# A written slot order for TensorE, VectorE and ScalarE in the message stage of a graph network kernel

## The chip, the core and the metric

The kernel runs on one core of a Trainium2 chip. The metric is the device time of one execution in microseconds (us). The kernel before takes 4433.76 us, the median of three timed runs that lie between 4427.78 and 4445.74 us. The profile is one more execution, taken by the hardware profiler; its span is 3774.9 us.

A core has five engines[...]: TensorE (PE in the profile: matrix products and transposes, results into PSUM), VectorE (DVE), ScalarE (ACT), GpSimd (POOL, which here issues the gathers by index) and SyncE (SP, which here issues the plain DMA transfers). [...]

## The reference

The input is a graph of 6250 nodes with 64 features and 206250 edges, sorted by destination. Four layers follow, each with a residual: x becomes x + layer(relu(layernorm(x))). The first, second and fourth multiply by the normalised adjacency matrix, with weights in the first, and three times in the fourth. The third layer is the one this study is about. Cut to what matters:

```python
Vp = leaky_relu(h @ pAw + pAb) @ pBw + pBb            # per node
x  = relu(relu(E @ w1 + b1) @ w2 + b2)                # per edge, E is 206250 x 64
msg = sigmoid(x @ Bw + Bb) * Vp[src] + (x @ Cw + Cb)  # per edge
M = clip(msg, 1e-5) ** 2
mean = segment_sum(M, dst) / max(count, 1)
out = sqrt(mean)                                      # per node
```

## The kernel before

The kernel first builds the 6272 x 6272 matrix of edge counts as bf16 tiles in device memory (`A`, 14 strips), multiplying by it as it goes, then makes two further products with it (to 1125 us in the profile), then does the third layer (**the message stage**), then the rest of the fourth layer's three products. A float32 operand of such a product is split into three bf16 terms (`split`), so that bf16 products sum to it.

**The message stage** is the loop at L1192. It goes over G = 202 groups of 1024 edges, that is J = 8 edges on each of 128 partitions. For one group:

- `v`: eight gathers by index on GpSimd (L1195), each fetching 128 rows of `Vp_dram`; four buffers.
- `e`: the edge features, one DMA on SyncE (L1199).
- `p_e`: four transposes on TensorE (L1203), copied out by ScalarE to `eT` (L1205).
- `p_1`, `h1`, `p_2`, `h2`: two products with block-diagonal weights (L1207, L1211), each taken out of PSUM by ScalarE with a relu (L1209, L1213).
- `p_bc`: gates and shifts, a product with the biases and one with the weights (L1216, L1220), over two PSUM banks.
- `gate`: a sigmoid on ScalarE (L1223).
- `m`: on VectorE the product with `v`, the shift and the clip (L1225 to L1227).
- `m3`: the square split into three bf16 terms, by ScalarE (L1229, L1230, L1232) and VectorE (L1231, L1233) in turn.
- `to`: VectorE's comparison of node numbers with the edges' destinations (L1238), a one-hot matrix over one or two blocks of 128 nodes.
- `p_s`: TensorE sums the messages into their nodes with it (L1246); a block that is complete is taken out to `H` (L1250). After each seventh block, `finished` does the square root, the residual and the layer norm of a chunk of 896 nodes.

**The matrix work beside it.** A list `todo` holds work on the adjacency matrix that does not depend on the group: `piece` loads a tile of `A`; `crossed` transposes a part of it on TensorE into the PSUM bank `p_sum` (L1136) and has VectorE compare it with the opposite tile (L1139), which is the check that the matrix is symmetric; `partial` multiplies a tile with a chunk that is complete (L732, called from L1144) and has VectorE add the result to `Y` (L1150, L1152), which is part of the fourth layer's first product. `p_sum` is one bank, so each of these must be read before the next begins. There are 196 `crossed`, 84 `partial` and 92 `piece` entries. `some_of` does a share per group, so that the list is empty when the next chunk is complete. The chunks' last groups are 29, 58, 87, 116, 145, 174 and 201.

**What sets the order.** The program names for each instruction its engine and its operands. A scheduler of the framework then fixes, at compile time, the order in each engine's queue from the dependencies and its own priorities, and adds the semaphores. PSUM has eight banks, and the stage uses all: `p_e`, `p_1`, `p_2`, `p_sum` one each, `p_bc` two, `p_s` two. SBUF tiles have three buffers each, `v` four. A tile can be written again when its last reader is done.

Of the kernel before, what the change touches and what calls it, by code (L numbers as in the profile page):

```python
# [8 lines left out]
F32 = mybir.dt.float32  # L9
BF16 = mybir.dt.bfloat16  # L10
FP16 = mybir.dt.float16
I32 = mybir.dt.int32
AF = mybir.ActivationFunctionType
OP = mybir.AluOpType
AX = mybir.AxisListType

P = 128
# [562 lines left out]

K1 = EP // P
LOOK = 101
NS = K1 // LOOK * P
# [11 lines left out]
def window(g):  # L597

    per = N / E
    lo = max(int(g * P * J * per) - DRIFT, 0) // P  # L600
    hi = min(int((g + 1) * P * J * per) + DRIFT, NP - 1) // P
    return lo, hi - lo + 1
# [3 lines left out]
def fast(ctx, tc, bad, x, src, dst, edge_attr, W3, b3, W4, b4, w1, b1, w2, b2, Bw, Bb, Cw, Cb,  # L606
# [432 lines left out]
    with ExitStack() as ph:  # L1039
# [83 lines left out]
        def crossed(n, i, k, b):  # L1123
            if b % ROWS == 0:
                held["there"] = mpool.tile([P, ROWS, 2, CW], BF16, name="there", bufs=2)
                m = min(ROWS, CB - b)
                for h in range(2):
                    nc.sync.dma_start(held["there"][:, :m, h, :],
                                      A[2 * i + h][:, k * CB + b:k * CB + b + m, :])

            p = ps_a.tile([P, 512], F32, name="p_sum").bitcast(BF16).rearrange(
                "p (a q) -> p a q", q=P)[:, :CB, :]
            for q in (slice(0, P),) if b != CB // 2 else (slice(0, D), slice(D, P)):
                half, lo = divmod(b * P + q.start, CW)
                for a in range(CB):
                    nc.tensor.transpose(p[q, a, :], held[half][:, a, lo:lo + q.stop - q.start],  # L1136
                                        ident_b)
            junk = mpool.tile([P, CB * P], BF16, name="junk", bufs=1)
            nc.vector.scalar_tensor_tensor(  # L1139
                junk, p.rearrange("p a q -> p (a q)"), 0.0,  # L1140
                held["there"][:, b % ROWS].rearrange("p h w -> p (h w)"), op0=OP.add,
                op1=OP.not_equal, accum_out=unlike[:, n:n + 1])

        def partial(i, s):  # L1144

            p = ps_a.tile([P, 512], F32, name="p_sum")
            for b in range(CB):
                spread(p, U3, i * CB + b, held[s % 2][:, b, :], CW, i * CB, CB)
            if i == 0:
                nc.vector.tensor_copy(Y[:, s, :], p[:, :CW])  # L1150
            else:
                nc.vector.tensor_add(Y[:, s, :], Y[:, s, :], p[:, :CW])  # L1152

        todo, crossings = [], []

        def plan(pairs, sums):
            order = [k for i, k in pairs] + [k for k in range(NC) if (pairs[-1][0], k) not in pairs]
            for at, (i, k) in enumerate(pairs if not sums else [(pairs[0][0], k) for k in order]):
                for half in range(2):
                    todo.append((piece, i, 2 * k + half))  # L1160
                    if sums:
                        todo.append((partial, i, 2 * k + half))
                    if at < len(pairs):
                        for b in range(3 + half) if not half else range(3, CB):
                            todo.append((crossed, len(crossings), i, k, b))
                            crossings.append((i, k, b))

        def some_of(left):

            n = -(-len(todo) // max(left, 1))  # L1170
            for _ in range(n):
                f, *args = todo.pop(0)
                f(*args)

        def finished(c):

# [12 lines left out]
        last = {b: g for g in range(G) for b in range(window(g)[0], sum(window(g)))}  # L1189
        ends = [last[c * CB + CB - 1] for c in range(NC)]  # L1190
        acc = {}
        for g in range(G):  # L1192
            v = mpool.tile([P, J, D], F32, name="v", bufs=4)
            for j in range(J):
                nc.gpsimd.indirect_dma_start(  # L1195
                    out=v[:, j, :], out_offset=None, in_=Vp_dram[:, :],
                    in_offset=bass.IndirectOffsetOnAxis(ap=src_g[:, g, j:j + 1], axis=0))
            e = mpool.tile([P, J * D], F32, name="e")
            nc.sync.dma_start(  # L1199
                e, edge_attr[g * P * J:(g + 1) * P * J, :].rearrange("(p j) f -> p (j f)", j=J))  # L1200
            p_e = ps_a.tile([P, 512], F32, name="p_e")
            for k in range(J // 2):
                nc.tensor.transpose(p_e[:, k * P:(k + 1) * P], e[:, k * P:(k + 1) * P], ident)  # L1203
            eT = mpool.tile([P, 512], F32, name="eT")
            nc.scalar.activation(eT, p_e, AF.Copy)  # L1205
            p_1 = ps_a.tile([P, 512], F32, name="p_1")
            nc.tensor.matmul(p_1, w1_d, eT, start=True, stop=True)  # L1207
            h1 = mpool.tile([P, 512], F32, name="h1")
            nc.scalar.activation(h1, p_1, AF.Relu, bias=b1_c)  # L1209
            p_2 = ps_a.tile([P, 512], F32, name="p_2")  # L1210
            nc.tensor.matmul(p_2, w2_d, h1, start=True, stop=True)  # L1211
            h2 = mpool.tile([P, 512], F32, name="h2")
            nc.scalar.activation(h2, p_2, AF.Relu, bias=b2_c)  # L1213
            p_bc = ps_a.tile([P, J, 2, D], F32, name="p_bc")
            for b in range(2):
                nc.tensor.matmul(p_bc[:, 4 * b:4 * b + 4].rearrange("p j o f -> p (j o f)"), ones,  # L1216
                                 BC_b, start=True, stop=False)
                for k in range(2):
                    q = 2 * b + k
                    nc.tensor.matmul(p_bc[:, 2 * q:2 * q + 2].rearrange("p j o f -> p (j o f)"),  # L1220
                                     h2[:, q * P:(q + 1) * P], BC, start=False, stop=(k == 1))
            gate = mpool.tile([P, J, D], F32, name="gate")
            nc.scalar.activation(gate, p_bc[:, :, 0, :], AF.Sigmoid)  # L1223
            m = mpool.tile([P, J, D], F32, name="m")
            nc.vector.tensor_mul(m, gate, v)  # L1225
            nc.vector.tensor_add(m, m, p_bc[:, :, 1, :])  # L1226
            nc.vector.tensor_scalar_max(m, m, EPS)  # L1227
            m3 = mpool.tile([P, J, 3, D], BF16, name="m3")
            nc.scalar.activation(m3[:, :, 0, :], m, AF.Square)  # L1229
            nc.scalar.activation(m, m, AF.Square)  # L1230
            nc.vector.tensor_sub(m, m, m3[:, :, 0, :])  # L1231
            nc.scalar.activation(m3[:, :, 1, :], m, AF.Copy)  # L1232
            nc.vector.tensor_sub(m3[:, :, 2, :], m, m3[:, :, 1, :])  # L1233

            some_of(min(k for k in ends if k >= g) + 1 - g)
            b0, nb = window(g)
            to = mpool.tile([P, 2 * P, J], BF16, name="to")
            nc.vector.tensor_tensor(  # L1238
                to[:, :nb * P, :], count[:, :nb * P, :],
                rel_b[:, g, :].unsqueeze(1).to_broadcast([P, nb * P, J]), op=OP.is_equal)  # L1240
            for b in range(b0, b0 + nb):
                begins = b not in acc
                if begins:
# [5 lines left out]
                if last[b] == g:  # L1249
                    nc.vector.tensor_reduce(  # L1250
                        H[:, b, :], acc[b][:, :3 * D].rearrange("p (t f) -> p f t", f=D),
                        axis=AX.X, op=OP.add)
                    if b % CB == CB - 1:
                        finished(b // CB)

        assert not todo and len(crossings) == 28 * CB

# [99 lines left out]
```

## Time and profile before

| stretch of the profile, us | what runs | length, us |
|---|---|---|
| 0 to 615 | building the matrix, first product | 615 |
| 615 to 1125 | two products with the matrix | 510 |
| 1125 to 3279 | message stage | 2154 |
| 3279 to 3775 | rest of the fourth layer | 496 |

| engine | busy in the whole span, us | share |
|---|---|---|
| TensorE | 3173.7 | 84% |
| VectorE | 1845.4 | 49% |
| ScalarE | 1329.9 | 35% |
| GpSimd | 1723.4 | 46% |

How to read what follows: a row of the costliest groups names the line, engine and operation, the tiles written and read, the count, the busy time and mean nanoseconds of one, and the idle time just before with what ended it. "issue" is idle time for which the profile shows no wait. A row of the timeline has the start, the duration, the engine and the operation, and in brackets the idle time before it and what ended that. A row of waits reads "who <- for whom", with the total, the number of times and the longest. [...]

### The profile page before, as it was taken

How to read it: one execution, taken by the hardware profiler on the slowest of the kernel's cores; microseconds unless marked ns; L12 is line 12 of the kernel's file. 1: busy time of each engine (PE TensorE's matmuls, PEld its weight loads, DVE VectorE, ACT ScalarE, POOL GpSimd, SP SyncE). 2: the span in 40 equal slices, each digit the busy share in tenths (PEclk: the TensorE clock that was granted, in tenths of full speed). 3: DMA queues.
4: the chain of work that ended last, by engine and by line, in shares of the span. 5: the costliest groups of instructions: out<-in, count | busy, mean ns of one | idle time of the engine just before them, and what ended most of it. 6: DMA issues, size and time to landing. Idle time of an engine off the chain costs nothing.

```text
span 3774.9 us, 59396 instructions
## 1 busy us (share of the span) xinstructions
PE 3173.7 (84%) x24499; PEld 1907.5 (51%) x24499; DVE 1845.4 (49%) x3013; ACT 1329.9 (35%) x2120; POOL 1723.4 (46%) x1822
## 2 busy tenths in 40 slices
PE   0499998999967777888878888888888888799999
PEld 0366665555534444444544444454444454466665
DVE  5999992221124445555555554555555455430000
ACT  0477771100104434334434434443443434310000
POOL 4100000000017777777777777777777777500000
PEclk9999998999978889889989889889899999899999
DMA  3244446968894333343434334333233333499987
GB/s 108 80 181 180 180 180 276 421 276 347 315 168 128 85 81 104 82 129 90 119 100 120 101 99 127 93 114 112 81 112 116 104 113 93 142 338 376 371 352 298
DMA packets 278031, 650.47 MB, mean 172 GB/s; under 512 B 106505, under 2 KB 158787, under 8 KB 275699
## 3 DMA queue, kind: packets, MB, share of 16 engines
q1 hardware_dynamic: 220036, 584.91, 42.9%
q0 software_dynamic: 54112, 58.92, 7.3%
q8 instruction: 194, 3.18, 0.3%
q10 hardware_dynamic: 3600, 2.73, 0.3%
q14 instruction: 89, 0.73, 0.1%
HBM read 562.82 MB, written 83.58 MB: 171 GB/s over the span
## 4 chain that ended last, share of the span: by engine, by line
POOL 32%; PE 15%; issue 12%; DMA 8%; DVE 2%; ACT 1%; POOLq 0%; DVEq 0%
POOL v L1195 32%; PE p_sum L732 11%; DMA v<-Vp_dram,src_g 7%; PE p_node L723 1%; PE p_bc L1220 1%; DMA piece<-A 1%; PE p L1207 1%; PE p L1211 0%; PE p_s L1246 0%; DVE m L1225 0%; PE p_sum L1136 0%; DVE junk L1139 0%; PE p_bc L1216 0%; DVE m L1226 0%; DVE m L1231 0%
## 5 line engine op out<-in xcount | busy, mean ns | idle before, releaser
L1195 POOL DMA_INDIRECT v<-Vp_dram,src_g x1616 | 1662.5, 1029 | 528.3 <-issue 455.2
L732 PE MATMUL p_sum<-piece,U 128*64 128x448 bf16 x10290 | 1083.7, 359 | 46.3 <-DVE junk L1139 22.9
L732 PEld LDWEIGHTS <-U 128*64 128x64 bf16 x12348 | 688.1, 111 | 610.8 <-issue 172.2
L1220 PE MATMUL p_bc<-BC,h 128*128 128x256 f32 x1616 | 507.5, 437 | 19.1 <-ACT h L1213 18.8
L1082 POOL MEMSET origin<- 128x4 f32 (+3 forms) x49 | 1.7, 100 | 968.3 <-PE p_sum L732 968.3
L1225 DVE TENSOR_TENSOR m<-gate,v 128x512 f32<-128x512 f32 x202 | 139.6, 691 | 510.9 <-DMA v<-Vp_dram,src_g 424.5
L1220 PEld LDWEIGHTS p_bc<-BC,h 128*128 128x128 f32 x1616 | 300.3, 207 | 173.7 <-issue 84.8
L1246 PE MATMUL p_s<-m,to 128*128 128x192 bf16 x2816 | 293.0, 259 | 73.8 <-DVE m L1233 73.7
L1246 PEld LDWEIGHTS <-to 128*128 128x128 bf16 x2816 | 270.6, 147 | 130.8 <-issue 124.3
L938 ACT ACTIVATE strip<-p_a 128x784 bf16<-128x784 f32 x392 | 301.6, 820 | 90.9 <-PE p_a L934 89.5
L1216 PE MATMUL p_bc<-BC_b,ones 3*128 3x512 bf16 x404 | 168.7, 418 | 190.0 <-DVE m L1226 188.4
L1229 ACT ACTIVATE m<-m 128x512 bf16<-128x512 f32 x202 | 126.9, 628 | 444.2 <-DVE m L1227 443.6
L1238 DVE TENSOR_TENSOR to<-count,rel_b 128x2048 bf16<-128x2048 bf16 (+1 forms) x202 | 218.8, 1084 | 101.8 <-PE p_s L1246 100.7
L973 ACT ACTIVATE y<-p_sum 128x448 f32<-128x448 f32 x56 | 30.5, 544 | 674.8 <-PE p_sum L732 674.8
L1207 PE MATMUL p<-eT,w_d 128*128 128x512 f32 x404 | 246.8, 696 | 25.3 <-ACT eT L1205 24.9
L1139 DVE SCALAR_TENSOR_TENSOR junk<-p_sum,there 128x896 bf16<-128x896 bf16 x196 | 213.1, 1087 | 78.6 <-PE p_sum L1136 69.9
L1211 PE MATMUL p<-h,w_d 128*128 128x512 f32 x404 | 240.7, 680 | 8.3 <-ACT h L1209 7.3
L1223 ACT ACTIVATE gate<-p_bc 128x512 f32<-128x512 f32 x202 | 120.6, 597 | 351.3 <-PE p_bc L1220 351.1
L925 DVE TENSOR_TENSOR lo<-count,key 128x2048 bf16<-128x2048 bf16 x196 | 238.2, 1215 | 0.0
L732 PE MATMUL p_sum<-strip,U 128*64 128x448 bf16 x2058 | 236.6, 358 | 0.4 <-ACT strip L938 0.4
L1231 DVE TENSOR_TENSOR m<-m,m 128x512 f32<-128x512 f32 x202 | 139.7, 691 | 168.8 <-ACT m L1230 168.8
L934 PE MATMUL p_a<-hd,lo 128*128 128x98 bf16 x3136 | 190.2, 214 | 33.1 <-DVE lo L925 31.8
(173 smaller groups left out, 3012.8 us busy)
## 6 DMA issues: line engine op xcount, KB each, us to landing
piece<-A SPq DMA_DIRECT2D x498, 784.0 KB
A<-strip SPq DMA_DIRECT2D x14, 5488.0 KB
e<-in_edge_attr SPq DMA_DIRECT2D x202, 256.0 KB
v<-Vp_dram,src_g POOLq DMA_INDIRECT x1616
there<-A SPq DMA_DIRECT2D x56, 448.0 KB
there<-A SPq DMA_DIRECT2D x56, 336.0 KB
pairs<-pair SPq DMA_DIRECT2D x1, 1616.0 KB
Vp_dram<-v SPq DMA_DIRECT2D x7, 224.0 KB
```

The costliest lines, as they stand in the source:

```text
L732: nc.tensor.matmul(p[half * D:(half + 1) * D, :w], U3[:, b, k, :], at_block, start=(i < 2), stop=(i >= 3 * n - 2))
L925: nc.vector.tensor_tensor(t, of.unsqueeze(1).to_broadcast(t.shape), key[:, k, at:at + GB].rearrange("p (h j) -> p h j", j=GQ) .unsqueeze(2 ...
L934: nc.tensor.matmul(p[:, j, :2 * NB], lo[:, g // GQ, :, g % GQ], hd[:, g // GQ, :, g % GQ], start=True, stop=True)
L938: nc.scalar.activation(strip[:, :, col:col + 2 * SG].rearrange("p b (j l) -> p b j l", l=2), p[:, :, :2 * NB].rearrange("p j (b l) -> p b ...
L1139: nc.vector.scalar_tensor_tensor(junk, p.rearrange("p a q -> p (a q)"), 0.0, held["there"][:, b % ROWS].rearrange("p h w -> p (h w)"), op0 ...
L1195: nc.gpsimd.indirect_dma_start(out=v[:, j, :], out_offset=None, in_=Vp_dram[:, :], in_offset=bass.IndirectOffsetOnAxis(ap=src_g[:, g, j:j ...
L1207: nc.tensor.matmul(p_1, w1_d, eT, start=True, stop=True)
L1211: nc.tensor.matmul(p_2, w2_d, h1, start=True, stop=True)
L1216: nc.tensor.matmul(p_bc[:, 4 * b:4 * b + 4].rearrange("p j o f -> p (j o f)"), ones, BC_b, start=True, stop=False)
L1220: nc.tensor.matmul(p_bc[:, 2 * q:2 * q + 2].rearrange("p j o f -> p (j o f)"), h2[:, q * P:(q + 1) * P], BC, start=False, stop=(k == 1))
L1238: nc.vector.tensor_tensor(to[:, :nb * P, :], count[:, :nb * P, :], rel_b[:, g, :].unsqueeze(1).to_broadcast([P, nb * P, J]), op=OP.is_equal)
L1246: nc.tensor.matmul(acc[b][:, :3 * D], to[:, (b - b0) * P:(b - b0 + 1) * P, j], m3[:, j].rearrange("p t f -> p (t f)"), start=(begins and j ...
```

## The change

The loop over groups becomes functions, one for each step, and a loop over slots calls them. In slot i each step works on another group: the transposes on group i, the first layer on i - 1, the second on i - 2, the gates on i - 3, sigmoid, clip and squares on i - 4 (`M_AT`), the sums into nodes on i - 5 (`SUM_AT`). So what a step needs from another engine was made in the slot before, with a few exceptions inside the slot. There are G + 5 slots. The whole loop stands in a region in which TensorE, ScalarE and VectorE issue in exactly the order in which the program names their instructions; GpSimd and SyncE are still the scheduler's. The matrix work is done in two shares a slot, and its reading by VectorE is put off to named places (`read_them`). The list's due times (`ends`) move by five slots, and a tile's `crossed` entries now come ahead of its `partial`. The edge features are loaded two slots ahead. Its aim is that no engine waits at the head of its queue for something that another has only just been given to do.

```diff
+ET = mybir.EngineType
...
+            def compared():
+                junk = mpool.tile([P, CB * P], BF16, name="junk", bufs=1)
+                nc.vector.scalar_tensor_tensor(...)
+            return compared
...
-        def some_of(left):
-            n = -(-len(todo) // max(left, 1))
-            for _ in range(n):
+        def some_of(n):
+            for _ in range(min(n, len(todo))):
                 f, *args = todo.pop(0)
-                f(*args)
+                if f is not piece:
+                    read_them()
+                then = f(*args)
+                if then:
+                    read.append(then)
...
+        BC_AT, M_AT, SUM_AT = 3, 4, 5
+        ends = [e + SUM_AT for e in ends]
...
-            nc.vector.tensor_sub(m, m, m3[:, :, 0, :])
-            nc.scalar.activation(m3[:, :, 1, :], m, AF.Copy)
-            nc.vector.tensor_sub(m3[:, :, 2, :], m, m3[:, :, 1, :])
-            some_of(min(k for k in ends if k >= g) + 1 - g)
...
+        def slot(i):
+            def at(later):
+                return 0 <= i - later < G
+            if i + 2 < G:
+                loaded(i + 2)
+            if at(3):
+                evicted(i - 3, "p_2", "h2", func=AF.Relu, bias=b2_c)
+            if at(M_AT):
+                gated(i - M_AT)
+                clipped(i - M_AT)
+            if at(0):
+                fetched(i)
+                turned_edges(i)
+            read_them()
+            if at(1):
+                layer(i - 1, w1_d, "eT", "p_1")
+            if at(M_AT):
+                squared(i - M_AT)
+            n = -(-len(todo) // max(min(k for k in ends if k >= i) + 1 - i, 1))
+            some_of(n - n // 2)
+            if at(M_AT):
+                compared_nodes(i - M_AT)
+                m, m3 = of[i - M_AT].pop("m"), of[i - M_AT]["m3"]
+                nc.vector.tensor_sub(m, m, m3[:, :, 0, :])
+                nc.scalar.activation(m3[:, :, 1, :], m, AF.Copy)
+            if at(2):
+                layer(i - 2, w2_d, "h1", "p_2")
+            if at(BC_AT):
+                gates_and_shifts(i - BC_AT)
+            if at(0):
+                evicted(i, "p_e", "eT", func=AF.Copy)
+            if at(1):
+                evicted(i - 1, "p_1", "h1", func=AF.Relu, bias=b1_c)
+            if at(M_AT):
+                nc.vector.tensor_sub(m3[:, :, 2, :], m, m3[:, :, 1, :])
+            read_them()
+            some_of(n // 2)
+            if at(SUM_AT):
+                summed(i - SUM_AT)
+
+        loaded(0)
+        loaded(1)
+        with tc.manual_schedule(engines={ET.PE, ET.Activation, ET.DVE}):
+            for i in range(G + SUM_AT):
+                slot(i)
+            read_them()
```

## The prediction

> **What bounds the kernel now.** I read the busy table by stage first, because the page's shares mix stages with different limits. Columns: stretch and length, busy time of TensorE, its weight loads, VectorE, ScalarE and GpSimd (each with a count), granted TensorE clock, DMA share, GB/s.
>
> ```profile
> 1125.00:3279.00 2154.00, 1775.79 (x9770) 1037.36 (x9771) 1130.31 (x1814) 895.28 (x1459) 1661.59 (x1616) 0.90 0.37 106
> 3279.00:3775.00 496.00, 469.89 (x4721) 287.87 (x4719) 75.80 (x131) 37.20 (x65) 0.83 (x1) 0.98 0.89 342
> ```
>
> The first row is the message stage, the only one the diff touches: 2154 of 3775 us. No engine looks full there: TensorE 82%, GpSimd 77%. Next the costliest group on GpSimd, on the page and then by itself (shortest, median, longest ns; first and last start):
>
> ```profile
> L1195 POOL DMA_INDIRECT v<-Vp_dram,src_g x1616 | 1662.5, 1029 | 528.3 <-issue 455.2
> L1195 POOL DMA_INDIRECT v<-Vp_dram,src_g x1616: 941/947/2005, 1124.9 to 3278.9; - x180
> ```
>
> The 1616 row gathers run from the first to the last microsecond of the stage, and their idle time is nearly all "issue", a wait for nothing. The GpSimd timeline shows what that is:
>
> ```profile
> 2212.14 0.95 POOL L1195 DMA_INDIRECT v<-Vp_dram,src_g  x1 [0.30 <-issue]
> 2213.39 1.50 POOL L1195 DMA_INDIRECT v<-Vp_dram,src_g  x1 [0.31 <-issue]
> 2215.20 0.95 POOL L1195 DMA_INDIRECT v<-Vp_dram,src_g  x1 [0.30 <-issue]
> ```
>
> Each gather is 0.95 us, with 0.30 us to the next, always. So GpSimd takes one every 1.25 us with no pause: 1616 x 1.25 = 2020 us, plus the lengthened ones (mean 1029 against median 947 ns, x 1616 = 133 us), gives 2153 of the 2154 us. GpSimd sets the stage, at 2154/202 = 10.66 us a group. The waits of the stage say the same from the other side (total, times, longest, us):
>
> ```profile
> DVE m L1225 <- DMA v<-Vp_dram,src_g: 423.1, 119, 8.1
> ACT m L1229 <- DVE m L1227: 439.7, 150, 7.9
> PE p_bc L1216 <- DVE m L1226: 188.4, 82, 7.0
> PE p_s L1246 <- DVE m L1233: 66.5, 32, 5.1
> ```
>
> VectorE waits for gathered rows, ScalarE for VectorE, TensorE for VectorE: one wait passed on. Last, how the stage ends:
>
> ```profile
> 3282.06 0.69 DVE L1225 TENSOR_TENSOR m<-gate,v 128x512 f32<-128x512 f32 x1 [1.42 <-DMA v<-Vp_dram,src_g]
> ...
> 3287.43 1.44 PE L1246 MATMUL p_s<-m,to 128*128 128x192 bf16 x8 [7.14 <-DVE m L1233]
> ```
>
> The last gather issues at 3278.9, its product starts 3.2 us later, the last sum 5.4 us after that.
>
> One thing the page does not explain: the timed runs take 4433.76 us against a profiled span of 3774.9, a factor of 1.17. [...] No run here shows the clock of the timed runs; I assume all engines slowed together, GpSimd still sets the stage, and a microsecond of the profile is worth 1.17 in the timed run.
>
> [...] 431 gathers with no VectorE operation beside them average 0.946 us; 71 with only the node comparison (L1238) beside them average 1.26. [...] the chain shows 2.4 us from issue to data again and again.
>
> **The change, part by part.**
>
> *GpSimd and DMA work.* The same 1616 gathers into the same four `v` buffers; the same loads. 0 us off the 2020 us floor.
>
> *The order on three engines.* No arithmetic is added or removed; per group TensorE does 1775.79/202 = 8.79 us, VectorE 1130.31/202 = 5.60, ScalarE 895.28/202 = 4.43, all under 10.66. What must be asked is whether the fixed order holds an engine longer than 10.66 us a slot. TensorE: from the first share of matrix work in a slot (it needs its `p_sum` bank read) round to the same place in the next lies one group's work, 8.79 us; it then waits about 1.9 us for VectorE to clip and read. VectorE: clip 0.69 + 0.68 + 0.46, a read of `p_sum` 1.17 (or 0.61), comparison 1.09, subtraction 0.69, ScalarE's copy 0.63 and about 0.15 of hand-over, subtraction 0.69: 6.3 us. ScalarE does nothing in a slot that it must wait for longer than that. Queued behind VectorE's wait for `v` are the `p_sum` reads, hence TensorE's matrix work, hence the gates: all delayed, none for longer than the gathers take. Cost in steady state 0; GpSimd's gathers hide it.
>
> *The distance of four slots to the product.* `fetched(i)` needs the buffer whose reader is `clipped(i-4)`. Three further buffers are 3 x 10.66 = 32 us of gathers; the product starts 2.4 us after its data's issue. About 29 us of slack. At the start, four buffers are free for 43 us from 1124.9, and slots 0 to 3 have at most 4 x 8.79 = 35 us of TensorE work. Cost 0, with 8 us to spare.
>
> *The ends of the seven chunks.* `finished` runs from L1250 to the last split in 10.6 us (3288.90 to 3299.52), and the written order puts the next slot's clip behind it. Within 29 us of slack, regained at 1.9 us a slot: 0. If none were hidden: 6 x 10.6 = 64 us.
>
> *The tail.* The last sum moves into slot 206, behind two more shares of the matrix work (a partial sum is some 2 us, a transposed comparison 0.7 us plus 1.17 of reading): 2 to 6 us, take 4; x 1.17 = 5.
>
> [...] Of the 133 us of lengthening the comparison makes most. It stays one per group, but its place after `v` arrives becomes nearly fixed, so its phase against the gathers is no longer spread. In the trace it lengthens gathers by some 0.1 us where it starts in the first 0.3 us of a gather's period and by 0.7 to 0.9 near its end; the slot's three possible places (0, 0.61 or 1.17 us of reading before it) fall in different phases. I take no change; ends -50 and +50 us.
>
> Sum: 4433.8 + 5 = 4438 us.
>
> **Rivals.** (1) [...] The same floor, and 2/5 of the 133 us go: 53 x 1.17 = 62, so 4376 us. For: the fixed place. Against: three phases average out. (2) *TensorE paces the timed runs.* If the factor 1.17 lies in TensorE's clock alone, 8.79 us a group becomes over 10.66 and its order counts. Its waits on ScalarE and VectorE outside the `p_bc` one sum to 184 us (66.5 on L1246, 25 on L1207, 26 on L1220 and L1211, 67 on `p_sum`); half of them x 1.17 = 108, so 4330 us. For: the granted clock of 0.90 here. Against: 0.96 to 0.99 in the other stretches, so the clock would have to fall everywhere. (3) *The written order costs.* Chunk ends unhidden and tail, (64 + 5) x 1.17 = 81: 4515 us. For: VectorE and ScalarE can no longer slip the next group's work between `finished`'s steps. Against: the 29 us of slack.
>
> **How the numbers follow.** Forecast 0.45, rival 1 0.17, rival 2 0.17, rival 3 0.21. Within 0.5% (22 us) lies most of the forecast's case: 0.42, with 0.02 to the faster side and 0.01 to the slower, so faster 0.36, slower 0.22. The range runs from 4320, which takes in rival 1 and half of rival 2, to 4515, which takes in half of rival 3; 0.08 + 0.10 are left out.
>
> **What would show it.** Right: 1616 gathers still 1.25 us apart with idle "issue" only, first to last start 2154 us apart within 25, the last sum 8 to 12 us after the last product starts. Rival 1: mean gather near 1.00 us. Rival 3: GpSimd waiting for VectorE (L1225) at chunk ends. Wrong altogether: a timed gain with a profiled gather stretch unchanged, which would mean that the timed runs are paced by something other than in the profile.

## The result, and the profile after

The changed kernel takes **4268.65 us** (median of four runs, 4252.64 to 4271.52) against 4439.75 us of the kernel before in the same series: ratio 0.9591, 95% interval 0.9523 to 0.9659. It is 171 us faster.

In some series of runs the kernel before takes about 3780 us and in others 4350 to 4450 us, all runs of a series alike, so kernels are compared only within a series. I call these the 3780 and the 4430 (or upper) level: the profile of before (3774.9 us) is of the first, and its timed runs, the timed runs of the changed kernel and the profile of after are of the second.

The busy table by stage of the changed kernel, with the columns of the prediction's first fence:

```profile
0.00:615.00 615.00, 460.03 (x5522) 300.99 (x5522) 518.11 (x865) 350.23 (x505) 51.98 (x59) 0.95 0.37 149
615.00:1125.00 510.00, 468.36 (x4482) 279.77 (x4483) 113.90 (x199) 47.18 (x91) 8.71 (x147) 0.95 0.87 316
1125.00:3770.00 2645.00, 1911.13 (x9735) 1117.82 (x9734) 1165.96 (x1821) 871.60 (x1448) 1632.38 (x1616) 0.80 0.32 86
3770.00:4267.00 497.00, 475.12 (x4762) 290.00 (x4762) 76.46 (x131) 36.59 (x64) 0.00 (x0) 0.98 0.89 343
```

Three stages last what they lasted before (615, 510 and 497 us). All of the excess over 3775 us lies in the message stage, 2645 us, and there VectorE, ScalarE and GpSimd have nearly the busy times of the profile of before (within 3.2%). What differs is idle time and the granted TensorE clock, 0.80 against 0.90. So the factor of 1.17 is not a slower clock of every engine.

The gathers, from the page's costliest groups and by themselves (shortest, median, longest ns, first and last start):

```profile
L1226 POOL DMA_INDIRECT v<-Vp_dram,src_g x1616 | 1632.4, 1010 | 1019.9 <-DVE m L1261 510.6
L1226 POOL DMA_INDIRECT v<-Vp_dram,src_g x1616: 939/945/1959, 1132.5 to 3748.0; - x180
```

A gather still takes 0.945 us, but GpSimd now waits 510.6 us for VectorE's product to free a `v` buffer, which it never did in the profile of before. TensorE's part of the timeline (PE its products and transposes, PEld its weight loads) shows another engine that is slow:

```profile
2297.33 0.14 PEld L1286 LDWEIGHTS <-to 128*128 128x128 bf16 x1 [1.97 <-issue]
2298.04 0.32 PE L1286 MATMUL p_s<-m,to 128*128 128x192 bf16 x1 [1.78 <-issue]
2298.77 0.15 PEld L1286 LDWEIGHTS <-to 128*128 128x128 bf16 x1 [1.29 <-issue]
2299.46 0.32 PE L1286 MATMUL p_s<-m,to 128*128 128x192 bf16 x1 [1.10 <-issue]
2300.16 0.18 PEld L1234 LDWEIGHTS p_e<-ident,e 128*128 128x128 f32 x1 [1.24 <-issue]
2300.86 0.37 PE L1234 MATMUL p_e<-ident,e 128*128 128x128 f32 x1 [1.08 <-issue]
```

One instruction starts every 0.70 us, whichever it is, and none waits for another engine ("issue"). In the stage TensorE has 546 idle times of over 0.15 us that no wait explains, 419 us in all; after 404 of them the instruction starts about 0.7 or 1.4 us after the one before. The profile of before, at the 3780 level, has two such idle times in the stage, of 5.9 and 0.4 us, both in its first 2.2 us.

### The profile page after: what moved, and what is told of

The parts are those of the page before. It is cut to its first block, busy times and chain, and to the rows that moved or that the text cites. A ratio compares the mean times of both kernels' runs of the same rounds, so it can differ in the third digit from the quotient of the medians.

```text
span 4266.6 us, 59486 instructions
## 1 busy us (share of the span) xinstructions
PE 3314.6 (78%) x24499; PEld 1988.6 (47%) x24499; DVE 1874.4 (44%) x3013; ACT 1305.6 (31%) x2108; POOL 1693.1 (40%) x1822
## 4 chain that ended last, share of the span: by engine, by line
PE 56%; DVE 13%; issue 13%; another core or an unknown queue 8%; ACT 4%; DMA 3%; POOL 2%; DVEq 0%; ACTq 0%; SPq 0%; POOLq 0%
PE p_sum L733 28%; PE p_bc L1252 7%; PE p L1238 6%; PE p_s L1286 5%; PE p_a L935 3%; PE p_bc L1248 2%; DVE junk L1143 2%; DVE m L1261 2%; PE p_node L724 2%; PE p_e L1234 2%; DVE m L1262 2%; PE p_sum L1137 1%; POOL v L1226 1%; ACT h L1242 1%
## 5 line engine op out<-in xcount | busy, mean ns | idle before, releaser
L1226 POOL DMA_INDIRECT v<-Vp_dram,src_g x1616 | 1632.4, 1010 | 1019.9 <-DVE m L1261 510.6
L733 PE MATMUL p_sum<-piece,U 128*64 128x448 bf16 x10290 | 1111.0, 368 | 194.9 <-issue 133.4
L733 PEld LDWEIGHTS <-U 128*64 128x64 bf16 x12348 | 721.5, 113 | 728.0 <-issue 254.3
L1252 PE MATMUL p_bc<-BC,h 128*128 128x256 f32 x1616 | 534.6, 451 | 57.7 <-issue 56.2
L1286 PE MATMUL p_s<-m,to 128*128 128x192 bf16 x2816 | 352.9, 279 | 119.4 <-issue 118.7
L1252 PEld LDWEIGHTS p_bc<-BC,h 128*128 128x128 f32 x1616 | 308.9, 212 | 206.9 <-issue 179.9
L1286 PEld LDWEIGHTS <-to 128*128 128x128 bf16 x2816 | 301.1, 150 | 178.3 <-issue 172.1
L1261 DVE TENSOR_TENSOR m<-gate,v 128x512 f32<-128x512 f32 x202 | 139.9, 692 | 503.9 <-ACT gate L1257 288.1
L1242 ACT ACTIVATE h<-p,b_c 128x512 f32<-128x512 f32 x404 | 262.4, 685 | 245.9 <-remote 172.5
L1238 PE MATMUL p<-h,w_d 128*128 128x512 f32 x404 | 254.7, 714 | 75.0 <-ACT h L1242 50.5
L1137 PE MATMUL p_sum<-ident_b,piece 128*128 128x128 bf16 (+1 forms) x1568 | 134.8, 235 | 209.8 <-DVE junk L1143 133.9
L1268 ACT ACTIVATE m<-m 128x512 bf16<-128x512 f32 x202 | 127.3, 630 | 505.8 <-DVE m L1263 398.4
L1137 PEld LDWEIGHTS <-piece 128*128 128x128 bf16 (+1 forms) x1568 | 108.5, 109 | 322.3 <-issue 265.9
L1238 PE MATMUL p<-eT,w_d 128*128 128x512 f32 x404 | 241.2, 679 | 16.4 <-issue 12.4
L1321 ACT ACTIVATE m<-m 128x512 bf16<-128x512 f32 x202 | 127.2, 630 | 370.3 <-DVE m L1320 285.7
```

The source lines that it names most:

```text
L733: nc.tensor.matmul(p[half * D:(half + 1) * D, :w], U3[:, b, k, :], at_block, start=(i < 2), stop=(i >= 3 * n - 2))
L1226: nc.gpsimd.indirect_dma_start(out=v[:, j, :], out_offset=None, in_=Vp_dram[:, :], in_offset=bass.IndirectOffsetOnAxis(ap=src_g[:, g, j:j ...
L1238: nc.tensor.matmul(of[g][p], w, of[g].pop(x), start=True, stop=True)
L1242: nc.scalar.activation(of[g][t], of[g].pop(p), **how)
L1261: nc.vector.tensor_mul(m, of[g].pop("gate"), of[g].pop("v"))
L1286: nc.tensor.matmul(acc[b][:, :3 * D], to[:, (b - b0) * P:(b - b0 + 1) * P, j], m3[:, j].rearrange("p t f -> p (t f)"), start=(begins and j ...
```

## The experiments

### First series: before again, the slots alone, and no gathers (3780 level)

`slots_scheduler_order` keeps the slotted program, but leaves the order on the engines to the scheduler:

```diff
-        with tc.manual_schedule(engines={ET.PE, ET.Activation, ET.DVE}):
-            for i in range(G + SUM_AT):
-                slot(i)
-            read_them()
+        for i in range(G + SUM_AT):
+            slot(i)
+        read_them()
```

The two "plain rows" kernels fill `v` with one plain transfer of fixed rows per group in place of the eight gathers, so that their messages are of other nodes:

```diff
-            for j in range(J):
-                nc.gpsimd.indirect_dma_start(...)
+            nc.sync.dma_start(v, Vp_dram[:P * J, :].rearrange("(p j) f -> p j f", j=J))
```

Expected of `before_again`, `slots_scheduler_order`, `before_plain_rows` and `after_plain_rows`:

> The kernel before, unchanged, profiled and timed once more. Theory S (slow stretches): the profile of the changed kernel shows stretches in which TensorE issues one instruction every 0.70 us with nothing to wait for, and the first profile of the kernel before (3775 us) shows none; its timed runs (4434 us) have them. Expected: profile near 4430 us, gaps of 0.7 us in the message stage as in the changed kernel or more of them, GpSimd waiting for L1225, all other stages within 1% of 615, 510 and 496 us. Theory C (one slower clock for all engines in the timed runs): profile near 4430 us with gathers of 1.1 us every 1.48 us and every VectorE operation 1.17 times as long, no such gaps.

> The changed kernel with the region of written order taken away: the same slots in the program, the order on the engines is the scheduler's. If the written order is what gains (theory W), this goes back to the kernel before: 4400 to 4500 us. If the staggering of the program and the later due times gain by themselves (theory P), it stays at 4230 to 4320 us.

> The kernel before with the same gathers left out and plain loads in their place. Theory G: 8.8 to 9.5 us a group, 3400 to 3550 us, no gaps of 0.7 us. Theory I: gaps as in the kernel before, 12 to 13.5 us a group, 4050 to 4350 us, and the difference to the changed kernel without gathers about as large as with them (150 to 200 us).

> The changed kernel with the eight gathers of a group left out: one plain DMA of the same size fills v from fixed rows, so the messages are of other nodes. GpSimd has no work in the stage. Theory G (the slow stretches come from GpSimd's gathers going on beside TensorE): no gaps of 0.7 us, stage near TensorE's own work, 8.5 to 9 us a group, 3350 to 3500 us in all. Theory I (they come from TensorE's own instruction stream): gaps stay, about 230 clear ones, stage at 10.5 to 12.5 us a group, 3750 to 4150 us.

Measured, with before at 3779.57 us: before again 3781.43 (ratio 1.0003, 0.9993 to 1.0012); the slots in the scheduler's order 3766.73 (0.9961, 0.9947 to 0.9975). Without gathers 3310.22 us for the program before and 3338.62 for the slots, one time each. The series was expected at the 4430 level and came out at the other, so the theories on the slow stretches, the written order and the gathers' part in them (S and C, W and P, G and I) were not decided by it. What it shows is the 3780 level: the gathers set the stage there, as the prediction said, since taking them out is worth 470 us. Without them the slots were 28 us slower (one run each), so their gain at this level seems to go through GpSimd and not through TensorE's order.

### Second: the changed kernel at the 3780 level

> The changed kernel, unchanged, beside the kernel before. In the last runs the kernel before took 3779.6 us and its profile again had no gaps of 0.7 us on TensorE. Theory E (the gaps belong to the conditions of a run, not to a kernel, and the gain is a gain under these gaps only): where the kernel before takes about 3780 us, the changed kernel has no gaps either, GpSimd's gathers run without pause for 2154 us again, and it takes 3765 to 3800 us, ratio 0.997 to 1.005; where the kernel before takes about 4435 us, 4250 to 4275 us, ratio 0.96. Theory K (the gaps come from the written order): the changed kernel takes about 4265 us also where the kernel before takes 3780, ratio 1.13.

Measured: 3750.24 us, before 3777.4; ratio 0.9927 (0.9914 to 0.9941), a gain of 27 us. That lies outside theory E's range at this level (0.997 to 1.005); theory K (1.13) is out. Its gathers and the end of its stage:

```profile
L1226 POOL DMA_INDIRECT v<-Vp_dram,src_g x1616 | 1630.2, 1009 | 528.0 <-issue 453.8 <-DVE missed L1094 35.8 <-DMA v<-Vp_dram,src_g 31.7
...
3252.01 0.69 DVE L1261 TENSOR_TENSOR m<-gate,v 128x512 f32<-128x512 f32 x1 [3.73 <-DMA v<-Vp_dram,src_g]
...
3261.04 0.88 PE L1286 MATMUL p_s<-m,to 128*128 128x192 bf16 x8
```

No wait for VectorE, as before; the mean gather is 1009 ns in place of 1029, x 1616 = 32 us. The excess of all gathers over 945 ns is 136 us in `before_again`, 118 in `slots_scheduler_order` and 105 here, and the first-to-last start 2154.8, 2134.5 and 2121.5 us.

The traces show how VectorE lengthens a gather. In `before_again` the 371 gathers during which a VectorE operation starts are at most 12 ns longer. A gather that starts while one runs is held, on average by 0.47 us in 170 cases of the node comparison, 0.17 us in 203 of the subtractions for `m3` and 0.10 us in 52 of the clip, and in no case by more than 1.05 us. Where that operation reads from PSUM (304 cases) it is held by 4 ns on average. So it matters which of the two starts first: in `before_again` a gather that starts second is held by up to 1.05 us, and one that has started is lengthened by at most 12 ns. From `before_again` to the changed kernel the comparison's part falls from 79 to 67 us, the subtractions' from 35 to 20 and the clip's from 5 to 0. So more comes from VectorE's other work than from the comparison.

The last sum ends 9.9 us after the last product starts, where it was 6.8.

### Third: a split comparison, and stalls put on TensorE (4430 level)

The split writes the node comparison in pieces of 64 nodes, so that each is short. The stall adds 72 products on TensorE in every eighth group or slot, into a `p_sum` bank, with results that nothing uses. That is some 15.4 us each time, as an estimate from the fourth series, where 2814 such products bring TensorE's busy time in the stage to 2216.85 us, from the 1615.22 of `before_plain_rows` at the same granted clock of 0.99: 0.214 us each. The two edits:

```diff
+            for k in range(0, nb * P, P // 2):
+                nc.vector.tensor_tensor(to[:, k:k + P // 2, :], count[:, k:k + P // 2, :], ...)
...
+            if i % 8 == 4:
+                p = ps_a.tile([P, 512], F32, name="p_sum")
+                for _ in range(72):
+                    nc.tensor.matmul(p, ident_b, count[:, :64, :]..., start=True, stop=True)
```

> The kernel before with the same split. Theory L: mean gather from 1029 to 990-1010 ns, 30 to 60 us faster, 3720 to 3750 us, and closer to the changed kernel with the split than 29 us. Theory D: 3775 to 3790 us.

> The changed kernel with the node comparison of a group (1.22 us for two blocks) written as four (or two) comparisons of 64 nodes, about 0.4 us each. Theory L (the 29 us that the changed kernel gains undisturbed are gathers held up less by VectorE's operations, and how long one operation holds GpSimd up grows with its own length): mean gather from 1009 to 980-992 ns, stage 30 to 45 us shorter, 3705 to 3725 us. Theory D (the 29 us come from the end of the stage or from TensorE): mean gather stays at 1005 to 1012 ns, 3745 to 3760 us.

> The kernel before with TensorE held up on purpose: in every eighth group 72 extra products of 512 columns (about 15.5 us at full clock), 25 times, some 390 us of added TensorE time whose result is not used. It stands for the stretches that the profile of the changed kernel shows (380 us of gaps of 0.7 us). GpSimd's floor has 10.67 - 8.79 = 1.9 us a group to spare, 380 us in all. Theory O (the order decides how much of TensorE's lateness the stage can take up): 250 to 450 us over 3780, more than the changed kernel with the same work by 80 us or more. Theory F (lateness costs both orders the same, and the recorded 4.1% came from one kernel having had worse luck): both rise by the same within 30 us.

> The changed kernel with the same 25 hold-ups, in every eighth slot ahead of the first layer's product. Theory O: 80 to 250 us over 3750. Theory F: the same rise as the kernel before with hold-ups, within 30 us.

Measured, with before at 4433.13 us: split before 4458.28 (1.0034, 1.0008 to 1.006), split after 4326.29 (0.9771, 0.9726 to 0.9815), stalled before 4754.37 (1.074, 1.0661 to 1.0819), stalled after 4565.31 (1.0313, 1.0239 to 1.0387). With the split the mean gather is 985 ns before and 992 after, against 1010 in the profile of after. The kernel before gains nothing by it, and the changed one shows no gain against the 4268.65 us of another series: one more sign that gathers don't set the time at this level. Theories L and D, written for the 3780 level, stay untested. The stalls cost 321 us before, and 297 after (against the same 4268.65), for 25 x 15.4 = 385 us of work. If that comparison of series holds, the kernels pass on nearly the same share; against the split kernel of their own series (4326.29) the stalls cost the slots 239 us, so this isn't settled. The stalled kernels are 189 us apart.

The profile of the split kernel before shows the old order at the 4430 level. Its L1139 is VectorE's read of a crossed transpose, its L1205 ScalarE's copy of `p_e` out of PSUM (an eviction), its L1207 the first layer; "remote" stands where the profile can't name the instruction that raised the semaphore:

```profile
1154.90 1.09 DVE L1139 SCALAR_TENSOR_TENSOR junk<-p_sum,there 128x896 bf16<-128x896 bf16 x1 [15.02 <-remote]
...
1156.05 0.91 PE L1136 MATMUL p_sum<-ident_b,piece 128*128 128x128 bf16 x7 [7.62 <-issue]
...
1164.78 0.60 ACT L1205 ACTIVATE eT<-p_e 128x512 f32<-128x512 f32 x1 [16.25 <-remote]
...
1165.43 2.08 PE L1207 MATMUL p<-eT,w_d 128*128 128x512 f32 x2 [8.47 <-issue]
...
1168.08 0.13 PEld L1136 LDWEIGHTS <-piece 128*64 128x64 bf16 x1 [0.33 <-issue]
1183.71 1.09 DVE L1139 SCALAR_TENSOR_TENSOR junk<-p_sum,there 128x896 bf16<-128x896 bf16 x1 [27.11 <-issue]
...
1184.87 0.37 PE L1136 MATMUL p_sum<-ident_b,piece 128*64 128x128 bf16 x2 [16.72 <-DVE junk L1139]
```

The seven transposes start at 1156.05; VectorE reads their result only at 1183.71, and in the last 15 us before that all engines but GpSimd stand still. The profile names VectorE as what TensorE waits for. But ScalarE and VectorE wait for TensorE's semaphore: it rises at 1154.88, 6.7 us after TensorE's last start and 0.02 us before the read at 1154.90, and at 1164.76, 8.1 us after the last start and 0.02 us before the eviction. (For the read at 1183.71 no rise is recorded; some are missing at this level. TensorE had then started nothing for 15.6 us.) So TensorE itself is late: its semaphore rises long after its last start (a **late report** below, from 1.5 us on). Whether the work was slow or only its report, the profile can't tell, since the ends of TensorE's operations are modelled. At the 3780 level no report in the stage comes over 1.08 us after TensorE's last start; here 216 of those recorded come over 1.5 us after it, up to 17.7 us.

### Fourth: more `v` buffers, and a copy of the lateness by hand (3780 level)

```diff
-            v = of[g]["v"] = mpool.tile([P, J, D], F32, name="v", bufs=4)
+            v = of[g]["v"] = mpool.tile([P, J, D], F32, name="v", bufs=8)
```

The stalls are those of the third series, with 42 products in every third group or slot.

> The kernel before with eight buffers for the gathered rows v in place of four, nothing else changed. In the 4458-us profile of the kernel before with the split comparison TensorE reported finished work up to 17.7 us after its last dispatch (216 reports over 1.5 us late, none in the 3778-us profile), and GpSimd stood still 119 times, 720 us in all, with `POOL v L1195 <- DVE m L1225` as its largest wait. Theory (lateness of TensorE reaches GpSimd through the four buffers of v): where the kernel before takes about 4430 us, eight buffers let GpSimd run some 40 us further ahead, its pauses fall under 250 us and the time to 4000-4150; where it takes about 3780 us it changes nothing (ratio 0.997 to 1.003), because GpSimd has no pause there. Rival (TensorE itself has too little slack left to catch up, so that it is the bound, whatever GpSimd does): within 1% of the kernel before on either chip.

> The slotted kernel with eight buffers for v in place of four. Theory (lateness of TensorE reaches GpSimd through the buffers of v): where the kernel before takes about 4430 us, GpSimd's 492 us of pauses fall under 200 us and the time from about 4268 to 3950-4100; where it takes about 3780 us, within 0.3% of the slotted kernel's 3750. Rival (TensorE is the bound there): 4220 to 4290 where the kernel before takes about 4430.

> The kernel before with 42 extra 128x512 products (about 9 us) on TensorE in every third group, 67 times, 610 us of TensorE in all; their result is not used. It copies by hand the lateness that the profiles of the slower chip show (about 70 stretches of 8 us median, 600 us in all). Theory (the order of the kernel before passes on nearly all of such lateness, since a late group holds up its own products, and these the buffers): on a chip where the kernel before takes about 3780 us it takes 4250 to 4450 us. Rival (lateness of TensorE is absorbed by its 18% of slack and is not what separates the kernels): 3850 to 4000. On a chip where the kernel before takes about 4430 us, both add up and TensorE becomes the bound: 4750 to 5000.

> The slotted kernel with the same 42 extra products in every third slot, 67 times, 610 us of TensorE in all; their result is not used. Theory (the slots absorb a part of the lateness that the order before passes on): on a chip where the kernel before takes about 3780 us, 100 to 250 us less than the stalled kernel before, where the two kernels without stalls differ by 28 us. Rival (the slots do nothing about lateness; what the first comparison showed came from elsewhere): 10 to 60 us less than the stalled kernel before. On a chip where the kernel before takes about 4430 us: 4600 to 4850, 100 to 250 us less than the stalled kernel before.

Measured, with before at 3780.26 us: eight buffers before 3780.52 (1.0001, 0.9992 to 1.001), after 3751.72 (0.992, 0.9903 to 0.9937), so the buffers bring nothing where GpSimd has no pauses (the changed kernel had 0.9927 with four). Stalled before 3914.71 (1.035, 1.0332 to 1.0367), stalled after 3996.05 (1.0569, 1.0551 to 1.0586). The order before takes some 600 us of extra work (2814 products of 0.214 us, as estimated above) for 134 us, inside the range of its rival, that TensorE's slack takes the lateness up. The slots pay 244 for it (against 3751.72), on the wrong side of both their theories. Plain extra work isn't a copy of what happens at the 4430 level. The message stage of the stalled kernel before and of the one with eight buffers shows one reason:

```profile
1125.00:3427.00 2302.00, 2216.85 (x12599) 1234.79 (x12599) 1148.83 (x1829) 894.68 (x1460) 1634.83 (x1616) 0.99 0.36 100
```

```profile
1125.00:3288.00 2163.00, 1779.57 (x9785) 1036.50 (x9785) 1137.17 (x1829) 899.41 (x1464) 1659.82 (x1616) 0.90 0.38 106
```

With the added products the granted clock is 0.99 where it was 0.90; at the 4430 level, in the profile of after, it is 0.80. TensorE is busy in 2216.85 of the 2302 us of the stalled stage, 96%.

### Fifth: the slots alone, and more buffers, at the 4430 level

> The slotted program without the hand-written order: the scheduler places the instructions of TensorE, ScalarE and VectorE. It took 3767 us (0.9961) on a chip where the kernel before takes 3780. Where the kernel before takes about 4430 us, theory A (TensorE sets the time there, since its instructions are late, and the written order keeps it from waiting for ScalarE's evictions of the same group): without the order most of the gain goes, 4370 to 4440. Theory B (the slots alone, that is the later product and the shifted chunk ends, bring it): 4250 to 4310. Where the kernel before takes about 3780 us: 0.995 to 0.998 again.

> The slotted kernel with eight buffers for v in place of four; 3752 us where the kernel before takes 3780. Where the kernel before takes about 4430 us, theory A (TensorE, occupied 2417 of 2652 us of the stage when its late reports and its gaps without a wait are counted, sets the time; GpSimd only waits for it): 4220 to 4290, as the slotted kernel with four. Theory C (the lateness reaches GpSimd, which still paces the stage, through the four buffers of v): 3950 to 4100. Where the kernel before takes about 3780 us: 0.990 to 0.994 again.

Measured, with before at 4448.03 us: the slots in the scheduler's order 4269.28 (0.9611, 0.9578 to 0.9644), the changed kernel with eight `v` buffers 4295.45 (0.967, 0.9629 to 0.9711). The first lies in theory B's range and not in A's: **the written order isn't needed, the slots bring the 4%.** The second is 5 us above the range for TensorE as the bound and far from the 3950 to 4100 us for GpSimd. With twice the buffers GpSimd waits as long for the products as before:

```profile
L1226 POOL DMA_INDIRECT v<-Vp_dram,src_g x1616 | 1630.5, 1009 | 1015.9 <-DVE m L1261 510.8 <-issue 449.8 <-DVE missed L1094 35.9
```

So the four buffers aren't the link, and GpSimd isn't what paces at this level.

### Sixth: the distances taken out

The scheduler's order again. `all_in_one_slot` lets every stage of group i stand in slot i; `layers_apart_only` keeps one slot between the transposes and each layer, and puts gates, product and sum together in slot i+3:

```diff
-        BC_AT, M_AT, SUM_AT = 3, 4, 5
+        BC_AT, M_AT, SUM_AT = 0, 0, 0
...
+            turned_edges(i)
+            evicted(i, "p_e", "eT", func=AF.Copy)
+            layer(i, w1_d, "eT", "p_1")
+            evicted(i, "p_1", "h1", func=AF.Relu, bias=b1_c)
+            layer(i, w2_d, "h1", "p_2")
...
```

> The slotted program in the scheduler's order with every distance taken out: edge transposes, both layers, gates, product and sum of group i all stand in slot i. The deferred reads of p_sum, the list of crossed transposes and sums and its split within a slot stay. Theory D (the distance between a group's stages keeps TensorE from waiting for ScalarE's evictions of the same group): the time of the kernel before, 0.995 to 1.005 of it, on either kind of chip, and where that takes about 4430 us TensorE waits over 280 us for others in the stage again. Theory R (the deferred reads and the new places of the crossed work bring the gain): 0.955 to 0.970 where the kernel before takes about 4430 us, 0.995 to 0.998 where it takes 3780.

> The slotted program in the scheduler's order with the distance kept for the layers alone: edge transposes in slot i, first layer in i+1, second in i+2, and gates, product and sum together in slot i+3. Theory D1 (the links between the edge layers are what cost the kernel before its time): as the slots, 0.955 to 0.970 where the kernel before takes about 4430 us, 0.995 to 0.998 where it takes 3780. Theory D2 (the distance from the gates to the product and from the product to the sum is what counts): 0.985 to 1.005 where the kernel before takes about 4430 us.

> The slotted program in the scheduler's order with every distance taken out, which took 0.9993 of the kernel before on a chip where that takes 3775 us. Where the kernel before takes about 4430 us, theory D (the distance between a group's stages brings the 4%): 0.990 to 1.005. Theory R (the deferred reads and the new places of the crossed work bring it): 0.955 to 0.970. Where the kernel before takes about 3780 us: 0.998 to 1.001 again.

Measured at the 3780 level, before 3774.53: all in one slot 3770.57 (0.9993, 0.9983 to 1.0003), layers apart 3767.75 (0.9987, 0.9975 to 0.9998). The second's expected 0.995 to 0.998 isn't met: there the distance of the layers is worth little. That the rest of the slots' 0.4% lies in the distance of product and sum is a guess from two series. In a later series, before at 4351.23: all in one slot 4355.3 (1.0009, 0.9981 to 1.0037). **Without the distances the 4% is gone**, though the deferred reads and the new places of the crossed work are still there; the due times of the matrix work, which follow `SUM_AT`, go back with them. Which of the distances does it at the 4430 level was not tried.

TensorE's waits (total, times, longest us) show the difference. L1238 is a layer's product, L1242 ScalarE's eviction of `eT`, `h1` or `h2`, L1252 the gates, L1286 the sum. All in one slot, at the upper level:

```profile
PE p_s L1286 <- DVE m L1317: 149.6, 25, 13.7
PE p_bc L1252 <- ACT h L1242: 94.0, 29, 11.2
...
PE p L1238 <- ACT eT L1242: 73.5, 24, 11.8
PE p L1238 <- ACT h L1242: 71.8, 36, 11.9
```

and the slots in the scheduler's order:

```profile
PE p L1238 <- ACT h L1242: 22.7, 9, 6.7
PE p_s L1286 <- DVE m L1331: 5.0, 3, 2.7
...
PE p_bc L1248 <- ACT h L1242: 2.2, 2, 1.2
```

Waits of TensorE for the link just before it in the same group add up to 389 us there and 30 here (432 in `before_split_to`); TensorE's own lateness, which comes back to it through the other engine, is in them.

### TensorE's account of the stage

Worked out from the traces: occupied is the time under any TensorE record, plus the time from its last start to a report of its semaphore, plus gaps that no wait explains; the rest of the stage it waits for others. Where a report is not recorded (25 to 59 in a profile at the upper level), the start of the VectorE or ScalarE instruction that waited for it stands for it. Late reports are those over 1.5 us after the last start, one for each such start, and the us that they make.

| kernel | level | stage us | occupied | waits for others | late reports, us in all |
|---|---|---|---|---|---|
| before_again | 3780 | 2163 | 1790 | 373 | 0 |
| all_in_one_slot | 3780 | 2162 | 1771 | 391 | 0 |
| slots_scheduler_order | 3780 | 2146 | 1768 | 378 | 0 |
| after_again | 3780 | 2134 | 1750 | 384 | 0 |
| before_split_to | 4430 | 2846 | 2557 | 289 | 98, 599 |
| all_in_one_slot_2 | 4350 | 2757 | 2518 | 239 | 106, 609 |
| slots_scheduler_order_2 | 4430 | 2623 | 2464 | 159 | 66, 316 |
| after (first profile) | 4430 | 2652 | 2422 | 230 | 56, 223 |
| after_v8_2 | 4430 | 2680 | 2444 | 236 | 53, 257 |
| before_stall9 | 3780 | 2299 | 2219 | 80 | 0 |
| after_stall9 | 3780 | 2377 | 2197 | 180 | 0 |

At the upper level TensorE's occupied time grows by 670 to 770 us for the same work and reaches 90 to 94% of the stage, where it was 82 to 83%. Of the 194 us between before_split_to and after, 135 are occupied time and 59 waits for others; of the 134 us between all_in_one_slot_2 and slots_scheduler_order_2, 54 and 80. These pairs are of different series. before_split_to and after_split_to are of one (stages of 2843 and 2708 us, 98 and 57 late reports of 598 and 233 us): by a count that takes every idle time ended by "issue" as occupied, 60 of their 135 us are occupied time and 74 waits. That count moves 45 to 70 us of the upper rows from the waits to the occupied time. Both take part, then, and the shares aren't settled. The "waits for others" of all in one slot, 239 us, are fewer than the over 280 us that theory D expected for the upper level.

## Why the prediction was wrong

**The step that failed** is the sentence "I assume all engines slowed together, GpSimd still sets the stage, and a microsecond of the profile is worth 1.17 in the timed run". It was my assumption, and no trace or run had shown it. The traces decide against it: a gather's median is 0.947 us at the 3780 level (the profile of before) and 0.945 at the 4430 level (that of after), the three other stages keep their length, and the excess is in the message stage alone, where TensorE slows. Every zero that was argued from staying under 10.66 us a group, behind the gathers, lost its cover with that step: at the 4430 level GpSimd stands still for 510.6 us of the stage, and there is no floor of gathers to hide behind. The prediction's own sign for being wrong altogether came true in substance: the timed gain was 171 us, where at the level of its profile the gathers' stretch shrank by 33.

**The right rival** was the second, TensorE paces the timed runs. Its objection, that the clock would have to fall everywhere, fails: from the profile of before to that of after it falls from 0.90 to 0.80 in the message stage, and in the others it is 0.99 and 0.95, 0.96 and 0.95, 0.98 and 0.98, with their lengths kept. But the clock alone, its stated cause, is too little: with it at 0.80 TensorE's busy time is 135 us longer (1911.13 against 1775.79), and the stage 491 (2645 against 2154). The rest is late reports, steps of 0.70 us and the waits that come of them. The rival's size was 108 us, half of TensorE's 184 us of waits in the profile of before, times 1.17; measured were 171. The term came from the wrong level: of the 184 us, 118 are waits for the link before, and in before_split_to these are 432.

**Where the forecast's own condition holds**, at the 3780 level, its steps can be held against the runs:

- *GpSimd and its work*: right. 1616 gathers 1.25 us apart, no pause; without them the time falls by 470 us.
- *Order, distance to the product, chunk ends at 0*: right. GpSimd hardly waits for L1261 (0.3 us in all).
- *Tail, +4 us*: right. The last sum ends 3.1 us later after the last product.
- *The lengthening of gathers, 0, ends ±50*: mis-sized. It fell by 31 us, and covers the whole gain (27 us, 0.7%). Rival 1 had the sign, and 53 us. First to last start became 2121.5 us, outside the 2154 ± 25 that was to show the forecast right. That the lengthening comes from VectorE's operations rests on which gathers are held, and for how long (second series); no run took these operations away by themselves, and by what means they hold a gather was not shown.

**What stays open.** Why TensorE slows at all at the upper level was not found: the same chip gave 3777 us in one series and 4351 in a later one. The lower clock does not show as the cause: in before_split_to the granted clock was full (1.0) at the start of 71 of the 96 recorded late stretches, and half (0.5) at the end of 64. Late loading of instructions does not show as the cause either: a transfer of the profile's kind "instruction" ended in only 8 of the 96. Whether the gathers take part is open, since the kernels without them were never run at this level; GpSimd is about as busy in the late stretches (58%) as in the stage as a whole (56%). Why the distances help there is shown in part: in one slot, the next instruction in TensorE's queue needs an eviction of the result that it has itself just reported late, so it starts nothing until the late report is in (98 and 106 late reports, 600 us); with the distances it has other groups' work to start, late reports are little more than half as many (53 to 66, 223 to 316 us), and a part of the slow stretches appears as its own gaps of 0.70 us. That TensorE's occupied time is shorter too, by 54 to 135 us, is measured and not explained. Against "slots always help a busy TensorE" stand the hand-made stalls: there they wait 180 us where the order before waits 80.

No kernel that was run beats the changed one at both levels. With the slots in the scheduler's order the upper level is the same (0.9611 and 0.9591, with overlapping intervals), and the written order is worth a further 0.3% at the lower one (0.9927 against 0.9961, in two series).

## What to carry to other kernels

When timed runs and profile differ by a factor, find out which stage and which engine the difference is in before scaling anything: a uniform factor would have kept the bound at GpSimd's gathers here, and TensorE's lateness moved it (GpSimd then waited 510.6 us). A wait that the profile puts down to the engine next in the chain can be the waiting engine's own lateness coming back, as in before_split_to, where TensorE's semaphore rose 6.7 and 8.1 us after its last start; look at when it rose. Putting the stages of a group one slot apart changed little here while another engine set the time (0.4 to 0.7%), paid 4% where TensorE was late by itself, and cost time where TensorE only had more work (244 us against 134).

## What was not expected of the hardware

- The same program takes 3762 to 3787 us or 4309 to 4482 us, by series. At the upper level TensorE's semaphore rises up to 25.2 us after its last start (after_v8_2), or it starts one instruction per 0.70 us, while gathers keep their median of 0.945 us and VectorE, ScalarE and GpSimd their busy times within 3.2% (after, against before).
- With work added to TensorE its granted clock was higher: some 600 us more of it cost the kernel before only 134 us, at 0.99 (before_stall9) in place of 0.90 (before_v8).
- A gather by itself takes 0.945 us (after; 0.946 in before), with 0.30 us to the next. One that starts while VectorE works on operands in SBUF can be held, by up to 1.05 us in before_again; one that has started is not (at most 12 ns), and work that reads PSUM holds hardly any (4 ns on average, in before_again).
